# A fused transformer block on one core: copies out of PSUM shared by two engines, a newly searched order, and another order of the experts

## The chip, the core and the metric

The kernel runs on one core of a Trainium2 chip. The core has a matrix engine (TensorE, PE in the profile, with its weight loads as PEld), VectorE (DVE), ScalarE (ACT), GpSimd (POOL) and a queue for transfers (SyncE, SP). Each engine works through its own list of instructions in the order in which the program gave them; where an instruction needs something that isn't there yet, everything behind it on the same engine waits too. [...] The metric is the device time of one execution in microseconds. The median of eight runs of the kernel before is 779.52 us (776.66 to 782.59).

## The reference

The input `x` is 16 sequences of 128 tokens with 256 numbers each; `ctx` has the same shape. Four blocks follow each other, each added to `x` behind a tanh gate:

```
x = x + tanh(g_xattn[0]) * attention(layernorm(x), ctx, ctx)       # softmax over features, 256 x 256 per sequence
x = x + tanh(g_ffn[0])   * ffn_sparse(layernorm(x))                # ternary weights, 1024 units, the top 10% kept, layernorm
x = x + tanh(g_xattn[1]) * conv(ctx, ctx, layernorm(x))            # products of ctx, a long convolution, gated by x
x = x + tanh(g_ffn[1])   * moe(layernorm(x))                       # 64 experts, 6 per token, 176 units each, plus a shared one
```

In the last block a softmax over 64 experts picks six for each of the 2048 tokens. An expert computes `silu(g) * u` on 176 units and projects back to 256 numbers, weighted by the token's share. A shared expert of 352 units sees every token.

## The kernel before

The program has two stages. **The front** does everything up to the routing. Tokens are worked on in eight pairs of sequences (`PAIR` = 2), and the pairs form five groups, `GROUPS = ((0, 1), (2, 3), (4, 5), (6,), (7,))`. A pair (function `pair`) goes through layernorm, `attention`, the sparse layer (`synapses`, `thresholds`, `answers`) and the layernorm of the third block. In `thresholds` the top 10% are found in six rounds: ScalarE counts with two sign passes over 128 x 1024 numbers (L1406), and VectorE makes the next threshold from the counts (L1414, L1418). A group (function `group`) then does the convolution: `products` multiplies context entries (`kv`, L1647, on GpSimd or VectorE), and `head` makes three matrix products for each of 16 heads and then multiplies and sums on VectorE (L1690, L1699). `routing` and `route` choose the experts and end with the slot numbers `at` (L1887, VectorE). With these, GpSimd stores every token's row six times in a table `slots_d` in DRAM, one indirect transfer per 128 rows and choice (L1892): 24 for a group of two pairs, 12 for one of one pair, 96 in all.

Copies out of PSUM stand at three places of the front and are all ScalarE's: the transposed tiles in `transposed` (L1284, 128x256, 64 of them), the kept units in `answers` (L1506, 128x512, 32) and the convolution's matrices in `setup_2` (L1194, 128x512, 8).

The order on each engine is written by a planner, the function `issue`. Every part of the front is a generator (a "stream") that yields operations with an engine, a cost in us, and what it reads and writes. The planner keeps a clock per engine, and at each step takes the operation that could start first, adding small handicaps: `leave(v, fn)` moves one operation later by `v` us in this comparison (or earlier, if `v` is negative), and `LATE_STREAMS` does so for a whole stream (stream 4 ranks the experts, stream 18 is the last group). With `either`, an operation has a second engine, and the one on which it would end first by the planner's clocks gets it; before, this holds for the products and sums of `pool_or_dve` (GpSimd or VectorE). None of this looks at the chip: the order is fixed when the program is built, and the handicaps are numbers in the source.

**The experts** come after. All 96 stores must have landed before the first expert's slots are read (`load_slots`). Experts are ranked by their number of tokens; rank 0 has the most, and `CAPS` says for how many slots each rank has room (384 for ranks 0 and 1, 320 for the next four, down to 160 for the last seven). The list `parts` holds the work in its order: from rank 63 (few tokens) down to rank 0. A rank with more than 256 slots has two parts, so there are 70. For each part, PE transposes the slots (L2132), VectorE copies them out of PSUM (L2137), PE makes the hidden units (L2161, L2177), ScalarE and VectorE apply silu and the product, PE projects back (L2197, L2198), ScalarE scales (`ys`, L2199), and GpSimd adds the rows to one of three sums in DRAM by an indirect transfer (L2081, `add_rows`). A part's sum is its rank modulo the number of sums that are still open; sum 2 is closed after part 51. Weights and slots are loaded by SP four parts ahead (`AHEAD`).

At the end the open sums are read back (`fold_load`, L2212) and added (`fold`, L2216), first the one that closed earlier, then the one of the last rank. Beside that, PE computes the shared expert for the last two pairs (L2228, L2244); VectorE's addition of that result (L2248) stands in its list between the folds of the last sum.

Of the kernel before, what the change touches and what calls it, by code (L numbers as in the profile page):

```python
# [10 lines left out]
ALU = mybir.AluOpType  # L11
# [4 lines left out]
P = 128  # L16
# [61 lines left out]
LATE_STREAMS = {4: 1.0}  # L78
# [530 lines left out]
def leave(late, fn):  # L609

    fn.late = late
    return fn
# [97 lines left out]
def fast_path(  # L710
# [133 lines left out]
    with ExitStack() as front:  # L844
# [136 lines left out]

        def pe(n, fn, reads=(), writes=()):
            return op("PE", 0.02 + n * 1.85e-3, fn, reads, writes)
# [78 lines left out]
        def setup():  # L1062
            V, A = nc.vector, nc.scalar
            yield ("wait", [event(("loaded", 0))])
            yield act(4, lambda: A.activation(tg, gates, AF.Tanh), [gates_m], [tg_m], "exp")
# [8 lines left out]
            for c in range(NC):  # L1074
                yield act(
                    N_SYN,
                    leave(-0.3, lambda: A.activation(sq, ws[:, c, :], AF.Square, accum_out=moments[:, c : c + 1])),
# [53 lines left out]
        def ternary(i, w_raw, q):  # L1131
# [17 lines left out]
            for unit, fn in (  # L1149
                (0.63e-3, lambda: V.tensor_scalar(q, w_raw, inv, 1.0, ALU.mult, ALU.min)),  # L1150
                (0.72e-3, lambda: V.tensor_scalar(q, q, -1.0, ROUND, ALU.max, ALU.add)),
# [3 lines left out]
            for o in (ALU.subtract, ALU.add):  # L1155
                if i:
                    for c in range(0, n_w, 512):
                        a, b = (flat(w)[:, c : c + 512] for w in (q, w_raw))
                        yield pool(512, leave(2.8, lambda: nc.gpsimd.tensor_tensor(a, a, b, o)), [m], [m])
# [10 lines left out]
        def setup_2():  # L1170
# [12 lines left out]
            for h0 in range(0, H, 2):  # L1183
# [8 lines left out]
                yield act(  # L1192
                    512,
                    lambda: A.copy(toe[:, h0 : h0 + 2].rearrange("p h k l -> p (h k l)"), b.ap),  # L1194
                    [b], [s],
# [16 lines left out]
        def norm(srcs, sm, reads):  # L1212
# [8 lines left out]
            for j in range(n):  # L1221
                yield dve(4, leave(-4.5, lambda: V.bn_aggr(mv[:, j, :], st[:, j, :])), [], [sm])
# [48 lines left out]
        def transposed(src, made, to, to_made, form="p (c t) -> p c t", **sizes):  # L1271
# [3 lines left out]
            for c in range(NC):  # L1275
# [6 lines left out]
            yield act(  # L1282
                D,
                lambda: nc.scalar.copy(to, b.ap[:, :D].rearrange(form, **sizes)),  # L1284
                [b], [to_made],
# [6 lines left out]
        def attention(p, j, xs, cs, q1, ctx, sums):  # L1292
# [8 lines left out]
            for c in range(NC):  # L1301
# [13 lines left out]
                2, lambda: nc.vector.tensor_scalar_mul(nmax, nmax, -(D**-0.5)), [sm], [sm]  # L1315
# [12 lines left out]
            for c in range(NC):  # L1328
                yield act(
                    S,  # L1330
                    leave(0.2, lambda: nc.scalar.activation(
                        vt.ap[:, c, :].rearrange("p (h i) -> p h i", h=H), turned_ctx[:, c],
                        AF.Copy, scale=den[:, c : c + 1],
                    )),
# [4 lines left out]
            for c in range(NC):  # L1339
                yield pe(  # L1340
                    D,
                    leave(-0.9, lambda: nc.tensor.matmul(
                        b.ap[:, :D], vt.ap[:, c, :], ex.ap[:, c, :],
                        start=(c == 0), stop=(c == NC - 1),
                    )),
# [44 lines left out]
        def thresholds(zs, sm, marked):  # L1390
# [10 lines left out]
            for k in range(len(GAINS) + 1):  # L1401
# [19 lines left out]
                else:  # L1421


                    fn = leave(1.0, lambda: V.tensor_scalar(
                        rank, seen_n, -0.5, TOP_SYN - 1.0 - 0.5 * N_SYN, ALU.mult, ALU.add
                    ))
# [10 lines left out]
            for j in range(n):  # L1437
                rest = yield ("get", rest_r)
                rests.append(rest)
                for cols, fn in (  # L1440
# [33 lines left out]
                        lambda: V.scalar_tensor_tensor(  # L1474
                            rest.ap, zs[j].ap, thr[:, j : j + 1], zs[j].ap, ALU.is_ge, ALU.mult
                        ),
# [13 lines left out]
        def answers(j, h1, kept, sums):  # L1490
            hid = yield ("get", hid_r)
            hid_t = hid.ap.rearrange("p (k t) -> p k t", k=NSC)
            for k0 in range(0, NSC, 4):
                b = yield ("get", banks)
                for k in range(4):
                    yield pe_turn(
                        lambda: nc.tensor.transpose(
# [3 lines left out]
                        ),  # L1501
                        [kept], [b],
                    )
                yield act(
                    512,
                    lambda: nc.scalar.copy(hid.ap[:, k0 * P : (k0 + 4) * P], b.ap), [b], [hid],  # L1506
# [4 lines left out]
            for k in range(NSC):  # L1511
                yield pe(
                    D,
                    leave(0.7, lambda: nc.tensor.matmul(  # L1514
# [859 lines left out]
```

## Time and profile before

| what | us |
|---|---|
| median of eight runs | 779.52 |
| the profiled execution's own time | 781.96 |
| its span, from the first to the last instruction | 780.2 |
| busy in the span: PE / DVE / ACT / POOL | 659.9 / 507.0 / 415.5 / 392.8 |
| last slot store of the front issued | 450.60 |
| first transpose of the experts | 457.32 |
| PE begins the shared expert | 750.82 |

An engine's busy time over the whole span says little here, since the two stages differ: in the front (0 to 452 us) PE, VectorE and ScalarE all work with gaps, and in the experts' stage PE has hardly any. So the profile is read by stretches, and in each stretch by what ended the waits. "<-" names who released the waiting instruction. Durations of neighbouring small instructions on VectorE and ScalarE overlap a little, so the sum of rows is larger than the busy time.

### The profile page before, as it was taken

How to read it: one execution, taken by the hardware profiler on the slowest of the kernel's cores; microseconds unless marked ns; L12 is line 12 of the kernel's file. 1: busy time of each engine (PE TensorE's matmuls, PEld its weight loads, DVE VectorE, ACT ScalarE, POOL GpSimd, SP SyncE). 2: the span in 40 equal slices, each digit the busy share in tenths (PEclk: the TensorE clock that was granted, in tenths of full speed). 3: DMA queues.
4: the chain of work that ended last, by engine and by line, in shares of the span. 5: the costliest groups of instructions: out<-in, count | busy, mean ns of one | idle time of the engine just before them, and what ended most of it. 6: DMA issues, size and time to landing. Idle time of an engine off the chain costs nothing. (4 is left out here: it accounts for less than half of the span.)

```text
span 780.2 us, 12529 instructions
## 1 busy us (share of the span) xinstructions
PE 659.9 (85%) x3254; PEld 520.8 (67%) x3254; DVE 507.0 (65%) x1824; ACT 415.5 (53%) x963; POOL 392.8 (50%) x365
## 2 busy tenths in 40 slices
PE   4566977896888887958898959999999998999993
PEld 2442455575575765747775548888888987887782
DVE  3895766999969996998976534444444453444554
ACT  5669799689896668366343114433433433333330
POOL 1271200240228521458587727776777776757640
PEclk9587998999799898987989979999999999999997
DMA  8999999755568856542133689999999998999566
GB/s 273 302 202 328 321 320 345 233 121 118 118 143 215 195 115 118 119 123 98 57 122 119 200 220 243 240 249 248 239 247 251 239 228 188 232 286 251 97 149 221
DMA packets 212623, 158.61 MB, mean 203 GB/s; under 512 B 121662, under 2 KB 197438, under 8 KB 212542
## 3 DMA queue, kind: packets, MB, share of 16 engines
q1 hardware_dynamic: 183342, 124.36, 58.4%
q0 software_dynamic: 25664, 29.96, 19.3%
q10 hardware_dynamic: 3536, 3.41, 1.3%
q8 instruction: 28, 0.46, 0.2%
q14 instruction: 53, 0.43, 0.2%
HBM read 92.24 MB, written 88.46 MB: 232 GB/s over the span
## 5 line engine op out<-in xcount | busy, mean ns | idle before, releaser
L2081 POOL DMA_INDIRECT acc_d<-ys,where x134 | 208.9, 1559 | 93.8 <-ACT ys L2199 70.9
L2199 ACT ACTIVATE ys<-epy,scale 128x256 f32<-128x256 f32 (+9 forms) x134 | 63.2, 472 | 144.0 <-PE epy L2198 142.0
L1892 POOL DMA_INDIRECT slots_d<-row,at x96 | 99.8, 1040 | 61.1 <-issue 52.7
L1406 ACT ACTIVATE seen<-shared_sb,small 128x1024 bf16<-128x1024 f32 x96 | 110.2, 1148 | 29.4 <-POOL small L1400 11.8
L2161 PE MATMUL epg<-xe,gu 128*112 128x256 f32 (+11 forms) x560 | 119.9, 337 | 0.6 <-DVE xe L2137 0.6
L2161 PEld LDWEIGHTS epg<-xe,gu 128*112 128x112 f32 x560 | 89.5, 178 | 10.9 <-issue 1.5
L2174 DVE TENSOR_TENSOR sa<-epg,sa 112x256 f32<-112x256 f32 (+9 forms) x70 | 25.4, 363 | 100.6 <-ACT sa L2173 99.2
L1671 PEld LDWEIGHTS bank<-kv,toe 128*128 128x128 f32 x480 | 77.4, 203 | 14.1 <-issue 9.3
L1671 PE MATMUL bank<-kv,toe 128*128 128x192 f32 (+1 forms) x480 | 84.5, 318 | 1.0 <-DVE pr L1690 0.7
L2197 PE MATMUL epy<-wa,sa 112*128 112x256 f32 (+10 forms) x268 | 80.8, 382 | 0.0
L2198 PE MATMUL epy<-wb,sb 128*128 128x256 f32 (+10 forms) x268 | 80.0, 379 | 0.1
L1374 PE MATMUL bank<-ws,ht 128*128 128x512 f32 x128 | 67.0, 635 | 5.6 <-ACT ht L1284 5.5
L2137 DVE COPY xe<-pxt 128x512 f32<-128x512 f32 (+9 forms) x70 | 39.8, 569 | 43.0 <-PE pxt L2132 42.8
L1690 DVE TENSOR_TENSOR pr<-bank,turned 128x128 f32<-128x128 f32 (+2 forms) x240 | 59.8, 290 | 8.3 <-PE bank L1671 7.7
L1514 PE MATMUL bank<-wo,shared_sb 128*128 128x256 f32 x256 | 63.9, 392 | 0.0
L1647 POOL TENSOR_TENSOR kv<-turned 128x256 f32<-128x256 f32 (+2 forms) x43 | 29.9, 720 | 60.7 <-PE bank L1671 60.6
L2177 PE MATMUL epq<-xe,gu 128*128 128x256 f32 (+11 forms) x280 | 59.6, 336 | 0.0
L2198 PEld LDWEIGHTS epy<-wb,sb 128*128 128x128 f32 (+10 forms) x268 | 45.1, 169 | 13.3 <-DVE sb L2186 0.5
L1514 PEld LDWEIGHTS bank<-wo,shared_sb 128*128 128x128 f32 x256 | 49.0, 198 | 5.9 <-issue 0.5
L2177 PEld LDWEIGHTS epq<-xe,gu 128*128 128x128 f32 x280 | 48.7, 193 | 1.5
L2132 PE MATMUL pxt<-ident,xt 128*128 128x128 f32 (+10 forms) x268 | 36.2, 256 | 12.5 <-DMA xt<-slots_d 12.5
L2132 PEld LDWEIGHTS pxt<-ident,xt 128*128 128x128 f32 (+10 forms) x268 | 31.2, 143 | 22.5 <-issue 13.3
(230 smaller groups left out, 1210.8 us busy)
## 6 DMA issues: line engine op xcount, KB each, us to landing
gu<-we_d SPq DMA_DIRECT2D x64, 352.0 KB
slots_d<-blank SPq DMA_DIRECT2D x2, 10432.5 KB
wa<-in_moe_w_dram SPq DMA_DIRECT2D x64, 112.0 KB
acc_d<-blank SPq DMA_DIRECT2D x3, 2176.0 KB
we_d<-in_moe_w_dram SPq DMA_DIRECT2D x96, 64.0 KB
fin<-acc_d SPq DMA_DIRECT2D x24, 256.0 KB
slots_d<-blank SPq DMA_DIRECT2D x1, 5216.2 KB
wb<-in_moe_w_dram SPq DMA_DIRECT2D x64, 64.0 KB
```

The source lines that it names most:

```text
L1374: lambda: nc.tensor.matmul(b.ap, ht.ap[:, c, :], ws[:, c, n0 : n0 + 512], start=(c == 0), stop=(c == NC - 1),),
L1406: lambda: nc.scalar.activation(seen.ap, zs[j].ap, AF.Sign, bias=at[:, j : j + 1], accum_out=seen_n[:, j : j + 1],),
L1514: leave(0.7, lambda: nc.tensor.matmul(b.ap[:, :D], hid_t[:, k, :], wo[:, k, :], start=(k == 0), stop=(k == NSC - 1),)),
L1671: lambda: nc.tensor.matmul(out_ap, toe[:, h, w, :], kvs[k], start=s[0], stop=s[1]),
L1892: put = nc.gpsimd.indirect_dma_start(out=slots_d, out_offset=bass.IndirectOffsetOnAxis(ap=at.ap[:, j, k : k + 1], axis=0), in_=rows[j].ap, ...
L2081: put = nc.gpsimd.indirect_dma_start(out=acc_d[r % n_open], out_offset=bass.IndirectOffsetOnAxis(ap=where, axis=0), in_=y, in_offset=None, ...
L2132: nc.tensor.transpose(pt[:, c, t, :q], slots[i][:q, t, c * P : (c + 1) * P], ident[:q, :q])
L2161: nc.tensor.matmul(pg[:FA, k, :m], gu[:, (k * NC + c) * FA : (k * NC + c + 1) * FA], xe[:, c, :], start=(c == 0), stop=(c == NC - 1),)
L2177: nc.tensor.matmul(pq[:, :m], gu[:, 4 * FA + c * P : 4 * FA + (c + 1) * P], xe[:, c, :], start=(c == 0), stop=(c == NC - 1),)
L2197: nc.tensor.matmul(py[:q, t, :], sa[:, at], wa, start=True, stop=False)
L2198: nc.tensor.matmul(py[:q, t, :], sb[:, at], wb, start=False, stop=True)
L2199: nc.scalar.activation(ys[:q, t, :], py[:q, t, :], AF.Copy, scale=scale[:q, t : t + 1])
```

## The change

There are three parts.

First, a new helper `act_or_dve`, which gives a copy out of PSUM to ScalarE or VectorE, whichever ends first by the planner's clocks. It is used at the three places named above. Second, the handicaps of the planner are other numbers at other operations; nothing is computed differently, but the order on every engine of the front is another one. Third, the experts: ranks 61 down to 0 come first, and ranks 63 and 62 (160 slots each) last. `sum_of` deals the parts to the sums by their place in this order, except that the last two ranks go into the same sum, number 1. The buffers of the second weight tile go by the same place.

```diff
-LATE_STREAMS = {4: 1.0}
+LATE_STREAMS = {4: 2.3, 18: 2.2}
...
+        def act_or_dve(n, to, src, reads, writes):
+
+            at_act = either(
+                lambda: nc.scalar.copy(to, src),
+                ("DVE", 0.12 + n * 1.0e-3, lambda: nc.vector.tensor_copy(to, src)),
+            )
+            return op("ACT", 0.17 + n * 0.83e-3, at_act, reads, writes)
+
...
-                yield act(
-                    512,
-                    lambda: A.copy(toe[:, h0 : h0 + 2].rearrange("p h k l -> p (h k l)"), b.ap),
-                    [b], [s],
+                yield act_or_dve(
+                    512, toe[:, h0 : h0 + 2].rearrange("p h k l -> p (h k l)"), b.ap, [b], [s]
                 )
...
-            yield act(
-                D,
-                lambda: nc.scalar.copy(to, b.ap[:, :D].rearrange(form, **sizes)),
-                [b], [to_made],
+            yield act_or_dve(
+                D, to, b.ap[:, :D].rearrange(form, **sizes), [b], [to_made]
             )
...
-                yield act(
-                    512,
-                    lambda: nc.scalar.copy(hid.ap[:, k0 * P : (k0 + 4) * P], b.ap), [b], [hid],
+                yield act_or_dve(
+                    512, hid.ap[:, k0 * P : (k0 + 4) * P], b.ap, [b], [hid]
                 )
...
+    def sum_of(r, n_open):
+
+        return max(E - 1 - turn_of[r], 1) % n_open
...
-            out=acc_d[r % n_open],
+            out=acc_d[sum_of(r, n_open)],
...
-    for r, n in reversed(list(enumerate(CAPS))):
+    by_turn = list(range(E - 3, -1, -1)) + [E - 1, E - 2]
+    turn_of = {r: i for i, r in enumerate(by_turn)}
+    for r in by_turn:
+        n = CAPS[r]
...
-        wb = wbs[r % len(wbs)]
+        wb = wbs[turn_of[r] % len(wbs)]
...
-    last_k = parts[-1][0] % len(still_open)
+    last_k = sum_of(parts[-1][0], len(still_open))
```

The handicaps change at these operations (before, after; a dash is none): the square of the quantized weights (-0.3, -), their gate's tanh (-, -0.8), the rounding step of the weights (-, -0.7), the sum of the second weights (2.8, -), the layernorm's aggregate (-4.5, -), the attention's maximum (-, -0.4), its value scaling (0.2, -) and its second product (-0.9, -), the last threshold's rank (1.0, -), the kept units (-, -0.6), their transposes (-, 1.2), their product (0.7, -), the routing's index row (0.1, -), its exponentials (-, -0.6), its marking (-, 0.2), its weights (0.4, -), its counts (-, 0.1), its slot numbers (-, -1.7), the slot stores (-0.6, 2.1), the experts' ranks (-, 2.2), and the shared expert's products (0.3, -), gating (-2.3, -) and sum (-2.9, 2.1).

## The prediction

> **What bounds the kernel now.** I read the page first, then the chain that ended last, then the busy time by stretches, then who waits for whom, then GpSimd's timeline around the end of the front.
>
> ```profile
> span 780.2 us, 12529 instructions
> PE 659.9 (85%) x3254; PEld 520.8 (67%) x3254; DVE 507.0 (65%) x1824; ACT 415.5 (53%) x963; POOL 392.8 (50%) x365
> PE 38%; DMA 2%; DVE 1%; issue 0%; ACT 0%; POOL 0%; SPq 0%
> ```
>
> The chain goes back only to the last slot stores of the front, and from there it is matmuls. So there are two stages with different limits: the experts (from 457 us on, PE) and the front before them, whose end is set by GpSimd's stores. Around that end the chain reads (start us, us, what):
>
> ```profile
> 449.32 0.97 POOL slots_d L1892
> 450.60 3.51 DMA slots_d<-row,at
> 454.31 2.88 DMA xt<-slots_d
> ```
>
> and the rows of the instruction that makes the slot numbers, and GpSimd's timeline just after it:
>
> ```profile
> L1887 DVE TENSOR_SCALAR at<-small x1: 182/182/182, 387.3 to 387.3; 128x32 int32<-128x32 f32 x1
> ...
> 388.29 0.99 POOL L1892 DMA_INDIRECT slots_d<-row,at  x1 [6.22 <-issue]
> ```
>
> 96 stores of 1.28 us each stand on GpSimd, and 48 of them belong to the last three routed groups. The third group's slot numbers (`at`, L1887) are ready at 387.3; GpSimd starts its first store at 388.29 and works almost without a gap to 451.57. So the front ends 64.3 us after the third `at`, and what delays that `at` delays everything. What it depends on is seen by stretches (columns: busy us of PE, PEld, DVE, ACT, POOL, then clock, DMA share, GB/s):
>
> ```profile
> 0.00:40.00 40.00, 19.80 (x60) 14.18 (x61) 24.41 (x85) 25.13 (x58) 7.95 (x21) 0.79 0.94 285
> ...
> 0.00:387.30 387.30, 300.41 (x1293) 219.06 (x1294) 318.25 (x1059) 283.64 (x642) 134.95 (x175) 0.89 0.74 194
> 40.00:387.30 347.30, 280.61 (x1234) 204.88 (x1233) 293.84 (x975) 258.52 (x585) 126.99 (x154) 0.90 0.71 184
> 160.00:200.00 40.00, 31.53 (x149) 24.53 (x147) 37.55 (x119) 35.02 (x69) 9.42 (x15) 0.91 0.58 117
> ...
> 160.00:387.30 227.30, 188.30 (x914) 147.99 (x913) 202.87 (x700) 157.70 (x346) 97.66 (x123) 0.91 0.57 129
> 80.00:240.00 160.00, 130.38 (x551) 92.04 (x550) 131.91 (x433) 140.67 (x316) 37.13 (x46) 0.93 0.80 214
> ```
>
> VectorE is the most loaded engine on the way to that `at` (84.6% from 40 us on), but between 80 and 240 us ScalarE is (88%). Who waits for whom from 40 to 388 us (us, times, longest):
>
> ```profile
> DVE small L1418 <- ACT seen L1406: 12.6, 12, 2.4
> ...
> ACT seen L1245 <- DVE small L1240: 24.8, 7, 10.4
> ...
> PE bank L1342 <- ACT vt L1331: 14.3, 11, 2.7
> PE bank L1277 <- ACT h L1265: 12.9, 8, 5.2
> ```
>
> VectorE's idle time ends with ScalarE's sign passes or with PE, and PE's in turn with ScalarE; but ScalarE waits for VectorE at least as much. The two engines are coupled.
>
> **The copies.** Instructions are counted in the order in which each kernel issues them. Of the 104 copies out of PSUM that ScalarE makes, 53 go to VectorE: 26 of 128x512 and 27 of 128x256, 28 of them in VectorE's first third. On ScalarE a wide one takes 0.575 us (row L1506), a narrow one 0.37 (L1284): 26 x 0.575 + 27 x 0.37 = 25 us less. VectorE's rows for the same kind are the experts' copies out of PSUM (L2137): 0.692 for 128x512 and 0.42 for 128x256. [...]
>
> **The order searched anew.** On VectorE, ahead of the third `at`: +26 wide and +25 narrow copies = 28.4 us; 15 products `kv` fewer, which GpSimd makes instead (5 x 0.92, 5 x 0.474, 5 x 0.30, row L1647 on VectorE) = -8.5; other small ones +2.7 (half a pair's norms, three sums); sum +22.6 us. In the whole front VectorE gets +19.5 and GpSimd +12.3 (17 products). ScalarE has 25 table loads for 23: 2 x 1.283 = 2.6 us more. ScalarE sat idle 88.8 of the 347.3 us, so the loads cost nothing; without that cover they cost their 2.6 us.
>
> GpSimd's order behind the third group's first store changes too: three stores of the second group and four `kv` products now stand among the others: 51 stores x 1.28 + 2 x 0.62 + 2 x 0.41 + 0.4 (index rows, memset), and 1.0 before the first = 68.7 us, where before it was 64.3. The last group's own 12 stores stand at the end, its `at` only some 30 us of VectorE work behind the third: 22 us early, so its later rank in the planner is hidden.
>
> So the new `at` needs 318.25 + 22.6 = 340.9 us of VectorE, 316.4 of them after the first 40 us (start-up, which waits for DMA and stays). To end the front at 451.6 as now, it must come at 451.6 - 68.7 = 382.9, that is, VectorE must be busy 316.4 / 342.9 = 92.3% from 40 us on, against 84.6% now. The order alone doesn't show which share it reaches, so I bound it. Lower end: the 89.3% of 160 to 387 us, where VectorE was already the bound; the 84.6% would be the old coupling with the ScalarE stretch. Upper end: 96%, half the idle share of its best stretch. I take 93.9%, the share from 160 to 200 us, because it is the row where VectorE had work queued while ScalarE too was near full; ScalarE itself goes from 74% to some 70%, and the early copies leave it in just the stretch where it bound. Then the third `at` comes at 40 + 316.4/0.939 = 377.0, the front ends at 445.7: **-5.9 us**.
>
> The new wait is on VectorE: a copy stands in its queue until PE's transposes end, and behind it stand the threshold steps (L1418) that the sign passes wait for. That is the price inside the share above.
>
> **The two experts last.** The same 64 experts with the same loads (weights three DMAs each, slots one or two) go through the same queues, permuted; PE's work is the same. Before, the last two experts take 735.5 to 750.8 us, the last 7.9 for 384 rows; two of 160 rows take 3.67 each (463.0, 466.7, 470.3 in the timeline) = 7.3. So the first open sum closes 7.3 instead of 7.9 us before PE's end, 0.6 later, and the last stores are four of 80 rows at 1.41 + 0.3 (6.8) instead of three of 128 at 1.54 + 0.3 (5.5), with less queued before them. Behind PE's end come 15.8 us of shared matmuls and then VectorE's last folds:
>
> ```profile
> 750.82 10.57 PE spg L2228 x48
> 761.39 5.19 PE spy L2244 x24
> 766.61 0.75 DVE L2248 SCALAR_TENSOR_TENSOR xs<-spy,tg,xs 128x512 f32<-128x512 f32 x1 [0.26 <-PE spy L2244]
> 767.28 3.40 DVE L2216 TENSOR_TENSOR xs<-xs,fin 128x512 f32<-128x512 f32 x5
> ```
>
> The last folds stand behind the shared part, not behind the sums: the loads have all been issued at 763.9. I price it at 0, between -1.4 (the last store stands 1.4 us in GpSimd's queue, 751.4 to 752.73, which could go) and +0.6 (the later closing, if the cover of 15.8 us were gone).
>
> **Sum.** -5.9 + 0 on the profiled execution: span 780.2 to 774.3, its time 781.96 to 776.1. That execution lies 2.4 us over the median of 779.52, so the median goes to **773.6 us**.
>
> **Rivals.**
> - *VectorE becomes the bound* (slower). The planner prices a wide copy on VectorE at 0.12 + 0.512 = 0.63 us where the row has 0.692, and a threshold step at 0.12 where its rows (L1418, L1431) have 0.29 and 0.31: its clock for VectorE runs early, and "ends first" picks the fuller engine. ScalarE's waits for VectorE, above, speak for it; against it, that ScalarE was the fuller one where most copies move. At 89.3%: `at` at 394.3, front at 463.0, +11.4: 790.9. At 84.6%: 414.0, +31: 810. It decides under 92.3%.
> - *Nothing to measure*: the shift and the longer row of stores cancel, 91.6 to 92.9%: 779.5, within 0.3% (2.3 us, about what a measurement of this kernel can tell).
> - *GpSimd's stores bound it from their start.* Group 0's `at` now stands behind 295 us of VectorE rows instead of 206 (rows that overlap a little: 375.5 of rows were 318.25 busy, so some 250 us). From the first store on GpSimd has 96 x 1.28 + 23.2 = 146 us. At 93.9% that `at` comes at 281 and the stores could end at 428: hidden by 18 us. It binds only if that `at` is later than 299; at 305 it alone gives the old end, 779.5.
> - *The experts' own stall*: PE waited 12.86 us of chain for one slot load at 649 (4 us idle). Another transfer order could lose or double it: 769.6 or 777.6 with the rest as forecast.
>
> **How the numbers follow.** Forecast (share 92.9 to 96%) 0.47 and better than that 0.03: faster 0.50. Cancelled 0.13. VectorE the bound 0.34 and GpSimd from its start 0.03: slower 0.37. The forecast's own range is 766 to 777. The whole range runs from 96% (`at` at 369.6, -13.3: 766) to 89.3% (791), which leaves out some 2 in 10.
>
> **What would show it.** Right: ScalarE down by some 20 us, VectorE up by some 19 in the front; the third `at` near 377, last slot store near 446, 68 to 69 us between them; VectorE at 93 to 95% from 40 us to that `at`; `ys` and `epy` rows unchanged, PE's end to the span's end still 29 us. Wrong: a third `at` behind 383 with ScalarE's waits for VectorE grown; GpSimd waiting between the stores of group 2 and 3; or an expert stage that is not 293 us from first transpose to the shared matmuls.

## The result and the profile after

The change made the kernel slower. The median is 794.33 us (792.35 to 799.27, 17 runs) against 780.44 us for the kernel before beside it (46 runs): a ratio of 1.0187, 95% interval 1.0169 to 1.0205. (Ratios here and below are those on record for the runs compared; they differ by up to 0.4% from the quotient of the two medians, which is 1.0178 here.) The profiled execution of after took 792.38 us with a span of 790.6; it lies 2 us under its median, and the one of before lay some 1.5 us over, so the two spans differ by 10.4 us where the medians differ by 13.9.

First the same stretches as before, up to the third `at` (now L1890), which came at 393.1 instead of 387.3. Columns: stretch and its length, busy us of PE, PEld, DVE, ACT, POOL, then clock, DMA share, GB/s.

```profile
0.00:393.10 393.10, 300.02 (x1286) 215.13 (x1287) 332.22 (x1107) 273.57 (x608) 134.98 (x190) 0.90 0.72 190
40.00:393.10 353.10, 281.97 (x1236) 202.38 (x1236) 305.83 (x1014) 250.16 (x550) 120.64 (x162) 0.91 0.70 180
160.00:200.00 40.00, 36.30 (x156) 26.43 (x156) 37.44 (x118) 25.03 (x54) 12.75 (x17) 0.96 0.58 116
160.00:393.10 233.10, 188.34 (x915) 144.48 (x916) 209.89 (x730) 151.80 (x334) 95.51 (x134) 0.93 0.55 125
80.00:240.00 160.00, 125.33 (x504) 87.20 (x503) 136.67 (x424) 127.70 (x271) 29.64 (x42) 0.89 0.79 208
```

VectorE was busy 86.6% from 40 us on (305.83 of 353.10), two points more than before, and not the 93.9% of the forecast. It worked 14.0 us longer up to the third `at` (332.22 against 318.25) and stood idle only 8.2 us less. ScalarE had less work, as forecast (273.57 us up to the third `at` against 283.64, and 397.0 over the whole run against 415.5), and in the stretch from 80 to 240 us it is no longer the fuller engine (127.70 against VectorE's 136.67).

The waits between 40 and 394 us (us, times, longest) show no new great one, and the coupling of VectorE and ScalarE is still there:

```profile
ACT seen L1410 <- DVE small L1422: 15.1, 10, 2.7
...
PE bank L1283 <- ACT row L1271: 11.1, 7, 4.3
...
DVE shared_sb L1386 <- PE bank L1378: 9.4, 9, 3.6
...
DVE small L1422 <- ACT seen L1410: 7.1, 7, 2.4
...
DVE small L1428 <- ACT seen L1410: 5.2, 4, 3.7
```

VectorE's waits for the sign passes hardly fell (12.5 us over its threshold lines, before 14.8), while the sign passes now wait more for the threshold step (15.1, before 11.3), and PE for the layernormed `row` (11.1, before 3.1; for the layernormed `h` it waits 10.0, before 12.9). The two lines of before for this:

```profile
ACT seen L1406 <- DVE small L1418: 11.3, 12, 1.9
...
PE bank L1277 <- ACT row L1265: 3.1, 5, 1.2
```

Added up over all rows of this view, ScalarE's waits that VectorE ended grew from 53 to 66 us, and VectorE's waits that ScalarE or PE ended fell only from 49 to 43. The price of the copies themselves was as forecast: 0.680 us for a wide one on VectorE and 0.418 for a narrow one (0.574 and 0.365 on ScalarE).

The chain that ended last goes through other things than before at both seams:

```profile
460.03 5.39 DMA slots_d<-row,at
465.63 2.99 DMA xt<-slots_d
...
760.69 10.37 PE spg L2239 x48
772.52 5.64 DMA fin<-acc_d
778.19 1.33 DVE xs L2227 x2
```

The last slot store was issued at 460.03 (before 450.60) and took 5.39 us to land, where before it took 3.51. At the end the last read of a sum stands in the chain, where before there was the second half of the shared expert's matmuls (`spy`). The 10.4 us of the spans are therefore: third `at` +5.8, the stores behind it +3.6 (67.9 instead of 64.3), from the last store to the first transpose +2.0 (8.7 instead of 6.7), the experts' stage -1.6, and the end +0.5.

### The profile page after: what moved, and what is told of

The parts are those of the page before. It is cut to its first block, busy times and chain, and to the rows that moved or that the text cites. A ratio compares the mean times of both kernels' runs of the same rounds, so it can differ in the third digit from the quotient of the medians.

```text
span 790.6 us, 12525 instructions
## 1 busy us (share of the span) xinstructions
PE 661.5 (84%) x3254; PEld 519.9 (66%) x3254; DVE 520.3 (66%) x1860; ACT 397.0 (50%) x912; POOL 396.4 (50%) x382
## 5 line engine op out<-in xcount | busy, mean ns | idle before, releaser
L2210 ACT ACTIVATE ys<-epy,scale 100x256 f32<-100x256 f32 (+10 forms) x134 | 63.2, 472 | 142.7 <-PE epy L2209 140.7
L1410 ACT ACTIVATE seen<-shared_sb,small 128x1024 bf16<-128x1024 f32 x96 | 109.9, 1145 | 26.3 <-DVE small L1422 15.1
L2172 PE MATMUL epg<-xe,gu 128*112 128x160 f32 (+11 forms) x560 | 119.9, 337 | 0.6 <-DVE xe L2148 0.6
L2208 PE MATMUL epy<-wa,sa 112*88 112x256 f32 (+10 forms) x268 | 80.9, 382 | 0.6 <-ACT ys L2210 0.6
L2209 PE MATMUL epy<-wb,sb 128*88 128x256 f32 (+10 forms) x268 | 79.9, 379 | 0.0
L1517 PE MATMUL bank<-wo,shared_sb 128*128 128x256 f32 x256 | 68.8, 399 | 7.9 <-ACT shared_sb L985 3.6
L2188 PE MATMUL epq<-xe,gu 128*128 128x176 f32 (+11 forms) x280 | 59.4, 335 | 0.0
L1598 POOL TENSOR_TENSOR h<-h,gam_b 128x256 f32<-128x256 f32 x6 | 6.7, 1124 | 104.4 <-ACT h L1271 88.9
L1517 PEld LDWEIGHTS bank<-wo,shared_sb 128*128 128x128 f32 x256 | 47.7, 200 | 16.3 <-ACT shared_sb L985 5.4
L1650 POOL TENSOR_TENSOR kv<-turned 128x256 f32<-128x256 f32 (+2 forms) x60 | 42.4, 736 | 25.7 <-PE bank L1674 25.6
L2209 PEld LDWEIGHTS epy<-wb,sb 128*88 128x88 f32 (+10 forms) x268 | 45.0, 169 | 13.1 <-DVE sb L2197 0.2
L1378 PEld LDWEIGHTS bank<-ws,ht 128*128 128x128 f32 x128 | 26.3, 221 | 34.9 <-issue 19.7
```

The costliest lines, as they stand in the source:

```text
L1378: lambda: nc.tensor.matmul(b.ap, ht.ap[:, c, :], ws[:, c, n0 : n0 + 512], start=(c == 0), stop=(c == NC - 1),),
L1410: lambda: nc.scalar.activation(seen.ap, zs[j].ap, AF.Sign, bias=at[:, j : j + 1], accum_out=seen_n[:, j : j + 1],),
L1517: lambda: nc.tensor.matmul(b.ap[:, :D], hid_t[:, k, :], wo[:, k, :], start=(k == 0), stop=(k == NSC - 1),),
L2172: nc.tensor.matmul(pg[:FA, k, :m], gu[:, (k * NC + c) * FA : (k * NC + c + 1) * FA], xe[:, c, :], start=(c == 0), stop=(c == NC - 1),)
L2188: nc.tensor.matmul(pq[:, :m], gu[:, 4 * FA + c * P : 4 * FA + (c + 1) * P], xe[:, c, :], start=(c == 0), stop=(c == NC - 1),)
L2208: nc.tensor.matmul(py[:q, t, :], sa[:, at], wa, start=True, stop=False)
```

## Experiments

The planner keeps a clock for each engine as it writes the order, and these clocks are part of the program. For the experiments the order that it wrote was recorded, as a list of (stream, engine) for all 2734 operations of the front, and given back to it. So the order and the engine of the copies can be changed one without the other:

```diff
-        times = {id(s): start_of(s) for s in ready}
-        s = min(
-            ready,
...
+        who, which = next(picks)
+        s = next(s for s in ready if s.id == who)
...
-        t, engine, cost, fn = times[id(s)]
+        t, engine, cost, fn = start_of(s, which)
```

`which` says on which engine the operation goes: 0 for the first one, 1 for the second. Where an experiment holds the order, the handicaps no longer play a part.

### The experts' order alone

```diff
-    for r, n in reversed(list(enumerate(CAPS))):
+    by_turn = list(range(E - 3, -1, -1)) + [E - 1, E - 2]
+    turn_of = {r: i for i, r in enumerate(by_turn)}
+    for r in by_turn:
+        n = CAPS[r]
```

and the lines of the change that belong to it (`sum_of`, `wbs`, `last_k`), on the front of before.

> The front of before, with the experts' order and sums of after (ranks 63 and 62 last, into sum 1). Forecast and theory 'front' (all of the loss is made before the first expert): the cost of this part was put at 0, between -1.4 and +0.6, so a ratio of 0.998 to 1.001 to the kernel before; the third slot numbers stay at 387 and the last store near 451. Rival 'experts' (the two experts last cost the end of the run several us, because the sum that closes last is read back later): ratio above 1.004, that is 3 us or more, all of it behind the last slot store.

Measured: ratio 1.0009, interval 0.9979 to 1.0038. The third `at` stood at 385.4, the last store at 449.3. The chain at the end does go through the last read of the sum here too:

```profile
751.42 8.65 PE spg L2236 x40
761.40 2.80 DMA fin<-acc_d
764.67 6.54 DMA fin<-acc_d
771.31 0.69 DVE xs L2224
```

but from the beginning of the shared expert to the end of the span it is 29.2 us (before 29.5). So this part is worth nothing that can be measured, and the whole loss is made before the experts. The read that is now in the chain is a bound that lies as late as the old one, not later.

### The order of after, all copies on ScalarE

`which` is 0 for the 104 copies, the rest of after's list is unchanged.

> The kernel after, with every instruction of the front issued in the recorded order of after, but all 104 copies out of PSUM on ScalarE as in before. Theory 'copies' (VectorE is overfull because of the copies, the new order by itself is harmless): VectorE loses 26 x 0.68 + 27 x 0.42 = 29 us of rows, the third slot numbers come at 385 or earlier, the total is 784 or less, ratio to before up to 1.005. Theory 'order' (the loss is the newly written order; the copies on VectorE help it): the copies go back to ScalarE, where the others wait for them; the planner's own clocks, with this order held, put the last store 28 us later than with the shared copies: 794 to 822, ratio 1.02 to 1.055.

Measured: 813.62 us, ratio 1.0396, interval 1.0344 to 1.0447, in the middle of what theory "order" gave, and the third `at` at 408.5, 15.4 us later than in after.

```profile
40.00:408.50 368.50, 289.40 (x1232) 204.60 (x1232) 284.44 (x964) 266.25 (x595) 118.75 (x162) 0.89 0.70 173
```

VectorE had 21.4 us less to do than in after up to that point (284.44 against 305.83) and came later. So theory "copies" falls: in this order the 53 copies on VectorE save time, and the order alone, without them, would cost 4%. Of the 32.0 us by which the span is longer than before's, 21.2 are there at the third `at`; 4.6 more come between the last store and the first transpose (11.35 us instead of 6.72).

### The order of before, the copies as in after, and chosen by the clocks

Both have before's list and `act_or_dve`. In the first, each copy has the engine that it has in after (53 on VectorE). In the second, each goes where it ends first by the planner's clocks in before's order; that made 31 copies on VectorE, 13 of them wide (the expectation said 30 and 14).

> The kernel before, with every instruction of the front issued in the recorded order of before, but the same 53 copies on VectorE as in after. Theory 'copies': the loss of after comes with them, third slot numbers at 393 to 400, total 790 to 797, ratio 1.012 to 1.021. Theory 'order': without the new order there is little loss: 778 to 784, ratio 0.997 to 1.005. The planner's own clocks, with this order held, put the last store 9.0 us later than in before, on the side of 'copies'.

> The kernel before, with every instruction issued in the recorded order of before, and each of the 104 copies on the engine where it ends first by the planner's clocks in that order: 30 copies go to VectorE (14 wide, 16 narrow), chosen for the order that is there. Theory 'copies' (each copy on VectorE costs its row, as VectorE is the most loaded): 30 copies put 16 us of rows on it, third slot numbers at 391 or later, ratio 1.005 to 1.012. Theory 'order' (a copy may go where the engine is free; the loss was the order): the planner's clocks put the last store 2.3 us earlier, ratio 0.995 to 1.000.

Measured: 783.93 us, ratio 1.0045 (1.0021 to 1.0069), and 778.9 us, ratio 0.9985 (0.9956 to 1.0014).

```profile
40.00:392.10 352.10, 281.62 (x1237) 204.86 (x1236) 314.10 (x1021) 241.59 (x540) 124.71 (x154) 0.91 0.73 181
```

That line is of the first: VectorE reached 89.2% there, with 20.3 us more work than before (314.10 against 293.84 from 40 us on), and the third `at` came only 4.8 us later, at 392.1. The ratio lies at the upper end of what theory "order" expected and far under "copies", though the third `at` is just short of the 393 that "copies" asked for. The 31 copies that were put where the clocks had room cost nothing that can be measured (0.9985); the 53 that were chosen for another list cost 0.45% (1.0045).

Beside after, which has the same 53 copies on VectorE, the first of these kernels shows where the order costs: at the third `at` the two are only 1.0 us apart (392.1 and 393.1), then after loses 3.4 us more in the stores and 1.9 more up to the first transpose. So the 5.8 us at the third `at` can't be shared out between copies and order. In the order of before the copies cost 4.8 and the new order then 1.0; with the new order first, the order costs 21.2 and the copies give 15.4 back.

### More copies on one engine

Before's list, and for the 53 copies a second one on VectorE (or on ScalarE) into a tile that nothing reads:

```diff
+        def twice(n, to, src):
+
+            nc.scalar.copy(to, src)
...
+            nc.vector.tensor_copy(out, src)
```

`out` is `spare` in the shape of the source. The other kernel has `nc.scalar.copy(out, src)` in the last line.

> The kernel before, in its own recorded order, where VectorE copies the 53 tiles that moved in after once more, behind ScalarE's copy, into a spare tile that nothing reads: 26 x 0.68 + 27 x 0.42 = 29 us of rows more on VectorE, nothing taken from ScalarE. Theory 'packed order' (the planner's list ties all engines to each other, so an added us on any of them costs most of itself): the last store comes 12 to 22 us later, ratio 1.015 to 1.028. Theory 'VectorE is the bound' (as the forecast's shares took it): 20 to 29 us, ratio 1.026 to 1.037, and nothing is to be had from ScalarE.

> The kernel before, in its own recorded order, where ScalarE makes the same 53 copies twice, the second time into a spare tile that nothing reads: 26 x 0.575 + 27 x 0.37 = 25 us of rows more on ScalarE, nothing added to VectorE. Theory 'packed order': the last store comes 10 to 20 us later, ratio 1.013 to 1.026; then relief of ScalarE is worth about what the load on VectorE costs, which is why before with the 53 copies moved lost only 0.45%. Theory 'VectorE is the bound': ScalarE sat idle 88.8 of 347.3 us, the copies go into that, 0 to 4 us, ratio 1.000 to 1.005.

In this batch, and in that of the two lists searched first, below, the kernel before itself ran at 810 and 805 us. No trace of it was kept there, but the traces of the other kernels of these batches show time lost late in the front. So their runs are read by their ratios, and their traces only up to the third `at`.

Measured: 1.0273 (1.0225 to 1.0322) with more on VectorE, 1.0116 (1.0073 to 1.0160) with more on ScalarE. Of 810 us that is 22.1 us for 29 us of rows on VectorE and 9.4 us for 25 on ScalarE. The third `at` says more: it came at 420.5 and 405.6, which is 33 and 18 us later than in the trace of before from another batch (the kernel after with the ranking's handicap changed back, below, ran in this batch; it has after's order up to there and had it 3.3 us later than after). So the price of work on ScalarE is only bounded: 0.38 us for each us by the ratio, 0.6 to 0.7 by the third `at`.

VectorE's number is not the price of work alone. The second copy reads the same bank (one of the program's eight PSUM tiles of 128x512, into which the front's matrix products write) as ScalarE's first one, and VectorE mostly stood idle ahead of it until that one was done (us, times):

```profile
  ACT shared_sb L1074: 10.9, 12
  ACT turned L1074: 9.7, 9
  ACT toe L1074: 4.5, 6
  ACT ht L1074: 3.8, 3
```

That is 28.9 us of waiting beside 29.1 us of copying. In the ScalarE kernel there is no such wait, but in both PE had to wait for second copies before it wrote the next products into their banks (6.9 us of PE's waits between 40 and 500 us ended with one in the VectorE kernel, 5.5 in the ScalarE kernel). The ratio with more on VectorE, 1.0273, lies within both theories' ranges (1.015 to 1.028 and 1.026 to 1.037), so it decides nothing. ScalarE's is more than twice what "VectorE is the bound" allows and a little under the lower end of "packed order". So the added work on ScalarE was not free (ratio 1.0116), though ScalarE was idle a quarter of the time (88.8 of 347.3 us in before), and taking copies from it should pay for a part of their price on VectorE; how large a part was not measured. The two numbers do not add up to the 3.5 us of the moved copies (22.1 - 9.4 = 12.7), and need not: a moved copy does not wait for a copy of ScalarE's.

### The ranking of the experts, late

In after the weight loads of the first experts were issued late. They wait for the ranking (stream 4, whose handicap the change raised from 1.0 to 2.3), and SP issues four experts' loads ahead of the first slots. SP's list in before (start, length, queue and line):

```profile
438.81 0.37 SPq L2107 DMA_DIRECT2D gu<-we_d  x1
...
447.72 0.48 SPq L2109 DMA_DIRECT2D wb<-in_moe_w_dram  x1
454.31 1.92 SPq L2115 DMA_DIRECT2D xt<-slots_d  x4
```

and in after:

```profile
454.27 0.37 SPq L2118 DMA_DIRECT2D gu<-we_d  x1
...
463.97 0.48 SPq L2120 DMA_DIRECT2D wb<-in_moe_w_dram  x1
465.63 1.91 SPq L2126 DMA_DIRECT2D xt<-slots_d  x4
```

In before SP was through 6.1 us ahead of the slot load and waited for the stores; in after it was through 1.2 us ahead, and the loads ran beside the last stores, the last of which took 5.39 us to land instead of 3.51. First the handicap was set back in after:

```diff
-LATE_STREAMS = {4: 2.3, 18: 2.2}
+LATE_STREAMS = {4: 1.0, 18: 2.2}
```

> The kernel after with one number changed back: the stream that ranks the experts has the handicap 1.0 in the planner again instead of 2.3. The order is the one of after up to the last 94 operations; then the ranks stand ahead of the last group's shared-expert work on PE and VectorE, by the planner's clocks 19 us earlier. Theory 'late ranks': in after the first experts' weight loads issue only from 454.3 on, against 438.8 before, since they wait for the ranks; they stand ahead of the first slot load in SP's queue and beside the last stores, whose landing takes 5.39 us instead of 3.51. Here they issue from 441 or earlier on, the landing is back to 3.4 to 3.7 us, the first transpose comes 6.7 us after the issue of the last store instead of 8.7, and the total is about 2 us under after: ratio to before 1.015 to 1.018. Rival (the landing only varies between executions, the loads are hidden): 8.7 us stay.

> The kernel after with the one number changed back (the ranking of the experts has the handicap 1.0 instead of 2.3), as in after_ranks, whose execution had standstills of 10 and 13 us late in the front that no engine ended. Theory 'late ranks': weight loads issue from 441 or earlier on instead of 454.3, the first transpose comes 6.7 to 7 us after the issue of the last store instead of 8.7, the total falls by about 2 us against after: ratio to before 1.015 to 1.018 for the 1.0187 of after. Rival (the landing varies by itself): 8.7 us stay.

Both runs of this kernel fell into the two batches with standstills: ratios 1.0220 (1.0172 to 1.0267) and 1.0240 (1.0158 to 1.0322), 11.0 and 10.1 us from the last store to the first transpose. The weight loads, expected from 441 on, were issued from 473.0 and 468.6 on. So these runs say nothing on the 2 us in question. The part that the handicap does not touch, the third `at`, came at 396.5 and 395.1 (after 393.1).

So the same number was changed in before instead, where the last store does not move:

```diff
-LATE_STREAMS = {4: 1.0}
+LATE_STREAMS = {4: 2.3}
```

> The kernel before with one number changed, the one that after changes: the ranking of the experts has the handicap 2.3 instead of 1.0. The first 2675 of 2734 operations keep their order; the ranks are then ready 13.0 us later by the planner's clocks. Theory 'late ranks': weight loads issue from 451 or later on (before: 438.8), beside and behind the last stores; the first transpose comes 8.5 us or more after the issue of the last store (before: 6.7), last store itself unchanged near 450 to 452, total 1.5 to 4 us longer: ratio 1.002 to 1.005. Rival (hidden): 6.7 us stay, ratio 0.999 to 1.001.

Measured: ratio 1.0086 (1.0060 to 1.0112). SP's list, and the first transpose:

```profile
449.20 0.37 SPq L2107 DMA_DIRECT2D gu<-we_d  x1
...
457.95 0.48 SPq L2109 DMA_DIRECT2D wb<-in_moe_w_dram  x1
458.91 1.91 SPq L2115 DMA_DIRECT2D xt<-slots_d  x4
```

```profile
463.18 0.76 PE L2132 MATMUL pxt<-ident,xt 80*128 80x80 f32 x4 [15.72 <-DMA xt<-slots_d]
```

The last store was issued at 449.58, as in before, but the slot load stood behind the weights until 458.9, and the first transpose came 13.6 us after the last store instead of 6.7. That is 6.9 us, more than expected; the medians differ by 7.4 (787.02 against 779.58). The rival is out for this order. In after the delay mostly hides behind the stores, which are late as well: SP was through with the weights at 464.45, before the last store landed at 465.42, and what is left of it, 2.0 us, is the longer landing. That the loads beside the stores lengthen the landing was not tested by itself; after's order with all copies on ScalarE, where the ranking stands as late, has 5.32 us too, and the four kernels with before's list and its early ranking (before, the experts' order alone, 53 and 31 copies on VectorE) have 3.46 to 3.66. If the loads stayed at their times, an earlier third `at` alone would gain an estimated 1 us at most in after, since the slot load stands behind them in SP's list and SP was through with them at 464.45, with the last store landed at 465.42.

### Lists that were searched further

From before's list, operations were moved, or their engine changed, one or two at a time, and a step was kept when the planner's clocks ended earlier. The kernels differ from before by `act_or_dve` and the list.

> The kernel before with act_or_dve and a new list of the front's 2734 operations: from the list of before, operations were moved and their engine was changed one or two at a time, and a step was kept where the planner's clocks (their costs also shaken by some per cent) ended earlier, 13,600 tries. 31 of 104 copies are on VectorE (14 wide). Planner's clocks: third slot numbers 377.6 (before 388.8), last store 445.2 (before 457.6). Theory 'order' (the time of the front is that of the list, and the planner's clocks follow it about as they did in the runs so far: planned +9.0 gave +5.0 us at the last store, planned -12.3 between after and before... -4.9 gave -9.4): last store at 439 to 446, ratio 0.983 to 0.994. Rival 'copies' (every copy on VectorE costs): slower than before or the same, 0.998 or more.

> The same search over the list of before (14,600 tries), with all 104 copies held on ScalarE. Planner's clocks: third slot numbers 384.9, last store 453.3 (before 457.6, best_copies 445.2). Theory 'a shared copy is worth something in a list that is made for it': between before and best_copies, ratio 0.990 to 0.999, at least 0.4% above best_copies. Rival (VectorE's copies bring nothing, only the list does): equal to best_copies within 0.3%.

The planned figures in the first of these stand for two pairs: 9.0 us planned between before and before with the 53 copies came out as 5.0, and 4.9 planned between before and after as 9.4. Measured: 0.9952 (0.9914 to 0.9990) with shared copies, 1.0053 (1.0018 to 1.0088) with all on ScalarE. The list without shared copies did not even keep up with before, although its clocks end 4.3 us earlier. Both lie above what was expected of them (0.983 to 0.994, which the first one's interval still touches, and 0.990 to 0.999). The two kernels differ by 1%, on the side of the theory that in a list made for it the shared copy is worth something; but they differ in the list as well as in the copies, so that part is not shown by itself.

> The kernel before with act_or_dve and the list of best_copies searched further (some 30,000 more tries): 34 copies on VectorE, 16 of them wide. Planner's clocks: third slot numbers 370.1, last group's 420.8, last store 437.4 (before 388.8, 441.1 and 457.6; best_copies 377.6, 428.1 and 445.2). best_copies was planned 12.4 us earlier at the last store and came out at a ratio of 0.9952. Theory 'order' (the chip follows the planner's clocks in part, as in the runs so far): 20 us planned give 5 to 14, ratio 0.982 to 0.994. Rival (the search now fits the planner's costs and not the chip): 0.994 to 1.000.

Measured: 770.11 us, ratio 0.9882 (0.9858 to 0.9906): faster than both kernels, and the last store 13 us earlier for 20 planned. Of the change it has the shared copies alone, 34 of them on VectorE; the order is another one, and the experts are as in before.

```profile
40.00:374.80 334.80, 277.08 (x1226) 201.22 (x1224) 296.44 (x964) 247.16 (x549) 144.97 (x185) 0.91 0.74 189
```

VectorE has 2.6 us more work than in before (296.44 against 293.84 from 40 us on) and 15.1 us less idle time (38.4 against 53.5).

### The planner's clocks beside the chip

All these from runs without standstills; "store" is the end of the last slot store, the share is VectorE's from 40 us to the third `at`.

| order / copies on VectorE | planner: third `at`, share, store | chip: third `at`, share, store | ratio |
|---|---|---|---|
| before / 0 | 388.8, 82.1%, 457.6 | 387.3, 84.6%, 451.6 | 1 |
| after / 53 | 390.7, 86.9%, 462.5 | 393.1, 86.6%, 461.0 | 1.0187 |
| after / 0 | 415.8, 75.3%, 490.5 | 408.5, 77.2%, 476.6 | 1.0396 |
| before / 53 as in after | 398.5, 86.5%, 466.6 | 392.1, 89.2%, 456.6 | 1.0045 |
| before / 31 by the clocks | 387.3, 85.7%, 455.3 | 388.5, 87.1%, 452.5 | 0.9985 |
| searched further / 34 | 370.1, 86.1%, 437.4 | 374.8, 88.5%, 438.1 | 0.9882 |

The program's own clocks already put after behind before, at the third `at` (1.9 us) and at the last store (4.9). They meet the chip's third `at` within 2% in every row, and VectorE's share within 2.7 points. They do not have all rows in the chip's order: after and before with 53 copies stand the other way round, and so do before and before with 31. Where they end and where the chip ends differs by up to 14 us.

## Why the prediction was wrong

**The failed step is the share of VectorE.** The forecast reads "I take 93.9%, the share from 160 to 200 us", worked the new `at` out as 377.0 and the front's end as 445.7. In the same 40 us VectorE again had 93.6% (37.44 of 40), but over the whole way it had 86.6%. In the forecast's own terms, VectorE was to stand idle for 20.6 us between 40 us and the third `at`; it stood idle for 47.3 (before 53.5), and 42.6 of these ended with ScalarE or PE. The coupling of the two engines, which the forecast took to be gone even at its lower end of 89.3%, was still there. A share from the best stretch was carried over to 337 us for which the order was there to be read: the planner's clocks have 86.9% for that order (they hit the chip's share more closely here than in any other row of the table). That share and the forecast's work would have put the third `at` at 404.1, some 11 us too late; nearer was the plain difference of the clocks between the two lists, +1.9 us there and +4.9 at the last store, for +5.8 and +9.4 measured. The argument behind the choice, that early copies free ScalarE and VectorE then has work queued, came out only for ScalarE: it did leave the stretch in which it bound, and VectorE's idle time went down by 8.2 us in all.

**VectorE's work** was estimated too high (over the whole run VectorE rose by 13.3 us where 19 were expected, and ScalarE fell by 18.5 where 20 were): 340.9 us up to the third `at`, measured 332.2. The rows rose by 17.9 (385.6 to 403.5; the prediction's 375.5 for before is not what the trace gives) instead of 22.6. The copies took 28.1 us, as foreseen. The `kv` products fell by 10.2 us instead of 8.5, and all other rows together stayed as they were where 2.7 more were foreseen, the threshold's start alone being 2.0 us shorter (columns as in the groups of the profile; before, then after):

```profile
L1431 DVE TENSOR_SCALAR small<-small,start 128x2 f32<-128x2 f32 x32 | 9.8, 306 | 0.4
...
L1647 DVE TENSOR_TENSOR kv<-turned 128x512 f32<-128x512 f32 x10 | 9.2, 917 | 0.0
```

```profile
L1435 DVE TENSOR_SCALAR small<-small,start 128x2 f32<-128x2 f32 x32 | 7.8, 245 | 0.3
...
L1650 DVE TENSOR_TENSOR kv<-turned 128x512 f32<-128x512 f32 x5 | 3.4, 679 | 0.0
```

The rest of the difference to the busy time, which rose by 14.0, is more overlap of neighbours. With the right work and the forecast's share the `at` would have come at 40 + 305.8/0.939 = 365.7, so the share alone missed by 27.4 us, and the error in the work hid 11.3 of them. The prices of single copies were right: the row that was taken, 0.692 us, lies 12 ns over the 0.680 of the trace.

**The fixed tail** was right: 68.7 us forecast from the third `at` to the end of the stores, 67.9 measured. The slack beside it was not: the last group's `at` was to come some 30 us behind the third and 22 us early, and came 48.0 us behind it, at 441.2, only 4.8 us ahead of that group's first store at 445.98.

**The ranking's handicap was not priced at all.** It was listed among the handicaps, but nobody asked what SP has queued behind it. The way from the last store to the first transpose grew by 2.0 us in after, and by 6.9 in before with that one number changed.

**The two experts last** were priced at 0, and are worth 0 (1.0009). The forecast's stage of 293 us was 291.8. That the last read of a sum would stand in the chain was seen as a bound of +0.6; the end took 0.5 us longer.

**The profiled executions.** The forecast of 773.6 lies 20.7 us under the measured median. In the profiled executions the miss is 16.3 us (776.1 forecast, 792.4 measured), 16.1 of it at the third `at`; the other 4.4 are where the two executions lie about their medians.

**The rivals.** "VectorE becomes the bound" at a share of 89.3% gave 790.9 us, nearest to the result, and the median of 794.3 still lies above the whole range, which ended at 791. Its sign came: a third `at` behind 383 with ScalarE's waits for VectorE grown (53 to 66 us). But its mechanism, copies that go to the fuller engine, holds only in the order of before, where they cost 4.8 us at the third `at`; with the copies back on ScalarE the order of after is 2% slower still. That the order could be poorer by itself, with or without copies, was not among the rivals. "GpSimd's stores from their start" had its turning point at 299 us; that `at` came at 298.9, and the first store of the third group still found GpSimd idle for 5.04 us, so it did not bind. "Nothing to measure" and "the experts' own stall" are out with the result and the 291.8.

**What stays open**: which of the changed handicaps makes the order poorer, and whether the late weight loads are what made the last landing longer in after. Setting one back writes a new order from that point on, so single ones can't be told apart in that way, apart from the ranking's, which acts only at the end. The group that comes first is routed 72 us later (298.9 against 226.5) for a second and third `at` at 333.1 and 393.1 (338.9 and 387.3); that shows what the order does, not which number did it.

## What to carry to other kernels

Where a planner writes the order, an engine's assignment has no price of its own: the same 53 copies cost 0.45% in one list and save 2% in another. So hold the list and swap the engine, then hold the engine and swap the list, before saying which of the two did it; and ask the planner's own clocks for the new list what share an engine will reach and which list ends first, rather than the best stretch of the old trace. They are no substitute for the run: two lists whose third `at` they put 7.8 us apart came out the other way round. For each operation that is moved later, look at what its reader has queued in front of others: a late ranking held up weight loads, and these the one load that everything waited for.

## What the hardware showed that was not expected

25 us of extra copies on ScalarE, an engine that was idle a quarter of the time, made the kernel 1.16% slower (9.4 of 810 us) and its third `at` came 18 us later than in before's trace from another batch.

In two of the four batches engines stood still late in the front with nothing that the profile names as awaited. In the second run of the ranking's kernel, between 380 and 500 us:

```profile
ACT seen L1251 <- issue: 28.1, 1, 28.1
...
DVE turned L986 <- remote: 15.9, 2, 14.9
DVE shared_sb L2010 <- issue: 13.2, 3, 7.4
ACT shared_sb L2006 <- issue: 12.4, 2, 9.6
```

Not all of this is new: ScalarE stood idle ahead of the same L1251 for 22.2 us in after too, where VectorE ended it, and ahead of the same L2006 for 9.3. New are VectorE's two rows, 14.9 us at the longest. The last group's `at` came 74.7 us behind the third there, in after 48.0. The same chip had run the kernel before at 779.7 us in an earlier batch. What held the engines was not found.

Some small instructions on VectorE took several times their usual length (up to 1.232 us, median 0.228) while GpSimd worked on elementwise products or sums. Of the 32 threshold operations on 128x2 (L1431), 26 took 0.206 to 0.230 us in before. The other six took 0.316 to 1.232 us; each began while GpSimd was at such an instruction, and ended 0.02 to 0.04 us after one of GpSimd's had ended. The longest:

```profile
342.99 0.63 POOL L1647 TENSOR_TENSOR kv<-turned 128x256 f32<-128x256 f32 x1
...
343.10 1.23 DVE L1431 TENSOR_SCALAR small<-small,start 128x2 f32<-128x2 f32 x1
343.56 0.74 POOL L1595 TENSOR_TENSOR h<-h,gam_b 128x256 f32<-128x256 f32 x1
```

In after two of the 32 were like that (0.456 and 0.625 us), and that is why the averages differ, 0.306 and 0.245 us, while the medians are 0.228 and 0.226. Beside GpSimd's indirect stores the same operation kept its length (0.219 us at 264.4 in before). The wide `kv` product shows it too: 0.675 to 0.684 us where GpSimd had no such work, and 0.806 to 1.670 where it had, the three longest at the start of before; the average of 0.917 us against 0.679 comes from those.
